# Message passing on one core: twelve of 556 edge tiles fetched row by row on two queues, an earlier merge of the third chunk, and later stores

## The chip, the core and the metric

The kernel runs on one core of a Trainium2 chip. The core has a matrix engine (TensorE, PE in the profile, with PEld for its weight loads), VectorE (DVE), ScalarE (ACT), GpSimd (POOL) and SyncE (SP). Each engine runs its own list of instructions in order and waits for the others by semaphores. SP, ACT and POOL can start DMA transfers; "SPq", "ACTq" and "POOLq" mark what their queues do. The metric is device time in microseconds (us), the median of several runs; lower is better.

## The reference

A graph layer with 12,500 nodes of 128 features and 400,000 edges, sorted by destination. For each edge no longer than 10 a filter is made from its length, multiplied into the projected features of the edge's source node, and summed at its destination; a small network, a residual and a layer norm follow.

```python
rbf = jnp.exp(-(distances[:, None] - centers) ** 2 / (2.0 * width * width))
cut = 0.5 * (jnp.cos(jnp.pi * distances / CUTOFF) + 1.0) * (distances <= CUTOFF)
W = (jax.nn.silu(rbf @ fw1 + fb1) @ fw2 + fb2) * cut[:, None]
messages = (h[src] @ pw + pb) * W
agg = jax.ops.segment_sum(messages, dst, num_segments=num_atoms)
out = h + (jax.nn.silu(agg @ mw1 + mb1) @ mw2 + mb2)
x = _layernorm(x + out)
```

Edge lengths are drawn up to 56, so that most edges fall away.

## The kernel before

**Packing.** The edges are taken in seven chunks (`pack_first`, `pack`). For each chunk VectorE shifts the short edges of each of 128 rows together, POOL scatters them to lists in DRAM (`packed`, line 494), SP reads the lists back (`pair`, `listed`, line 821), and VectorE merges three lists into one (`one_of`, lines 839 and 840). The merged list holds source and place of each edge; TensorE turns it (line 902), and VectorE copies it to `srci` (line 907), the table of source indices. The lengths are merged in `lengths` and stored to `near_d` (line 896). All this is `unpack`.

**Quads.** The 556 tiles of 128 edges that remain are worked in 139 quads of four tiles (`NL = 139`). For a quad: POOL fetches the projected source rows of a tile with one indirect DMA each (`fetch`, line 1048; the first 12 quads fetch `x` itself and are projected later); ACT makes the radial basis (`basis`, lines 1094 and 1095) and a silu (`silu`, line 1109) for a pair of quads, `oct` by `oct`; TensorE multiplies (`first`, line 1103; `second`, lines 1117 and 1120); VectorE multiplies filter and source rows (`message`, lines 1129 and 1131) and builds a one-hot matrix (`place`, line 1143); TensorE sums by destination (`sum_up`, line 1163) and VectorE adds that to the table `aggT` (`add`, line 1196). I call the engines that work on a quad after its fetch "the consumers".

**Tiles by rows.** For the quads in `SINGLY` the first of the four tiles is not fetched by POOL. SP starts 128 DMAs of one 512-byte row each instead (`one_by_one`, line 1038), after reading 32 addresses at a time into registers (line 1034), into one of four slots of `dl_0`.

**Nodes.** From quad 70 on, blocks of four tiles of finished nodes are worked in between (`nodes`): load `x` (line 173), `node_first`, `node_second` (line 1205 and 334), `node_stats`, then for four blocks together `deviations` (a Sqrt on ACT, line 1241) and `scales`, and `normalize` (line 1263 on ACT), which also stores the block on SP (line 173). `tail` and the last lines do this for the last blocks, with `keep_busy` issuing matmuls that nobody reads (line 1352).

**What sets the order.** The order on each engine is written out by the Python code. A planner keeps an estimated time (`clock`), an estimated time of POOL (`pool`, 1.29 us a fetch), and for each chunk the time before which its next step is not put in (`awake`); `pack_until` puts steps of chunks between quads. A row of `one_by_one` is planned at `A_ROW` us. A fetch waits for the sum of a quad four before the newest one written (`FOLLOW`), and for its buffer (`place_of`: 21 buffers at first, for later quads reused after four to six quads).

Of the kernel before, what the change touches and what calls it, by code (L numbers as in the profile page):

```python
# [67 lines left out]
CLEAR_C = 2  # L68
PACK_US = 1.5
EARLY_US = 7  # L70
SINGLY = (22, 45, 62, 67, 86, 102, 118, 133)
A_ROW = .58
AT_ONCE = 32
FROM_BANK = 3


# [7 lines left out]
def kernel(  # L84
# [56 lines left out]

    x_sb, loaded = {}, [0]

    def load_x(t0, n=None):
        t = x4_sb[loaded[0] % X_BUFS]
        loaded[0] += 1
        node_dma(t0, t, x, False, n)
        x_sb[t0] = t
# [293 lines left out]
    def fetches(until, most):  # L442

        while fetched[0] < QT * min(most, known[0]) and pool[0] <= until:
            q, j = divmod(fetched[0], QT)
            fetch(q, table=x if q < FROM_X else None, js=(j,))
            if j == 0:
                pool[0] = max(pool[0], summed.get(before_it(q), 0.0))
            if j or q not in SINGLY:
                pool[0] += 1.29  # L450
            there_at[q] = pool[0] + 2.2
            fetched[0] += 1

    def parts(n):

        return [(a, b) for a, b in ((0, n // 16 * 16), (n // 16 * 16, n)) if b > a]
# [236 lines left out]
    def pack(c):  # L693
# [109 lines left out]
            yield one(n)  # L803

        yield from columns(c, nodes, r_d, first, 0, CAP, at_i)
        awake[c] = pool[0] + (2.2 if c == 1 else 3.0)
        awake[0] = 0.0
        yield 0
        yield from unpack(c)
# [1 line left out]
    def unpack(c):  # L811
# [15 lines left out]
        if c < 2:  # L827
            more_ = np_ if c == 0 else SPILL
            also = work.tile([P, 2, QE], F32, name="s", bufs=3).bitcast(I32)
            listed(also, 0, more_, 3, LISTS)  # L830
        awake[c] = max(awake[c], clock[0]) + (6 if c < 1 else 3.5 if c < 2 else 4.0)
        yield 0
        def alike_in(k):
            nc.vector.tensor_tensor(pair[:more_, :LISTS - 3, k::2], pair[:more_, :LISTS - 3, k::2],
# [2 lines left out]
        def one_of(to, k):  # L837

            nc.vector.tensor_tensor(to, pair[:np_, 0, k::2], pair[:np_, 1, k::2], OP.bitwise_or)
            nc.vector.tensor_tensor(to, to, pair[:np_, 2, k::2], OP.bitwise_or)  # L840
# [49 lines left out]
        def lengths():  # L890

            if c < 2:
                alike_in(1)
            one_of(length, 1)
            for a, b in parts(np_):
                nc.sync.dma_start(near_d[p0 + a:p0 + b], length[a:b].bitcast(F32))
            stored.add(c)

        def to_places(f, to):
            t, tp = turned()  # L900
            for j in range(2):
                nc.tensor.transpose(tp[:, j, :np_], f[:, j * P:(j + 1) * P], ident[:np_, :np_])
            if to is srci:
                lengths()
                yield 1.4 if c < 2 else 0.8
            yield later(-2.0 if c == 1 and to is srci else 0.0)
            nc.vector.tensor_copy(to[:, p0:p0 + np_, :].rearrange("p r j -> p j r"),
                                  tp[:, :, :np_])
            back(t)
# [5 lines left out]
            pool[0] = max(pool[0], clock[0] + 0.4)  # L915
        known[0] = QB[c + 1]
        yield 0
        mine = [q for q in SINGLY if QB[c] <= q < QB[c + 1]]
        if mine:
            at_row = work.tile([64, P], I32, name="at_row", bufs=2)  # L920
            nc.vector.tensor_scalar(at_row[:np_], f_src[:, :P], float(4 * H), None, op0=OP.mult)
            for q in mine:
                p = 2 * (q - QB[c])
                singles.extend((q, e, at_row[p:p + 1]) for e in range(P))
# [100 lines left out]
    def one_by_one():  # L1025

        row_at[0] = max(row_at[0], clock[0] - 8.0)
        while singles and row_at[0] < clock[0]:
# [4 lines left out]
            if e % AT_ONCE == 0:  # L1033
# [5 lines left out]
                              proj.rearrange("n f -> (n f)").bitcast(U8)[ds(rows_at[e % AT_ONCE], 4 * H)]  # L1039
                              .rearrange("(o f) -> o f", o=1))  # L1040

    def fetch(q, idx=None, table=None, js=range(QT)):
        got = quad_sb[place_of(q) if q >= 0 else 0]
        for j in js:
            if q in SINGLY and j == 0:
                continue
            i = srci[:, 2 * q + j // 2, j % 2:j % 2 + 1] if idx is None else idx[:, j:j + 1]
            ins = nc.gpsimd.indirect_dma_start(  # L1048
                out=got[:, j, :], out_offset=None, in_=proj if table is None else table,
                in_offset=bass.IndirectOffsetOnAxis(ap=i, axis=0))  # L1050
# [73 lines left out]
    def message(q, js=(0, QT)):  # L1124
        msg = own(q, "msg", 0)
        a, b = js
        if q in SINGLY and a == 0:
            assert q in alone and all(s[0] != q for s in singles)
            nc.vector.tensor_mul(msg[:, 0, :], pu_of[q][:, :H], alone.pop(q))
            a = 1  # L1130
        nc.vector.tensor_mul(msg[:, a:b, :], pu_of[q].rearrange("p (j f) -> p j f", j=QT)[:, a:b, :],  # L1131
                             got_of[q][:, a:b, :])
        if b == QT:
            free.append(pu_of.pop(q))
            got_of.pop(q)
        return msg
# [115 lines left out]
            ready.append((t, r[:, at:], by[:, at:]))  # L1252
            at += len(rows(t))

    def normalize(t0, rs, by, on=(), eng=nc.sync):

        y = x_sb.pop(t0)
        for k, m in enumerate(rows(t0)):
            if k in on:
                nc.vector.tensor_scalar(y[:m, k, :], y[:m, k, :], rs[:m, k:k + 1], by[:m, k:k + 1],  # L1260
                                        op0=OP.mult, op1=OP.add)
            else:
                nc.scalar.activation(y[:m, k, :], y[:m, k, :], AF.Identity, bias=by[:m, k:k + 1],  # L1263
                                     scale=rs[:m, k:k + 1])
        node_dma(t0, y, out, True, eng=eng)

    ready = []

# [25 lines left out]
    assert begin[early[-1]][2] <= NL - 3  # L1294

    def nodes(q):

        if deep:
            scales(*deep.pop())
        for _ in ready[:1 if q < NL - 6 else 2]:  # L1300
            normalize(*ready.pop(0))
        for k, t0 in enumerate(early):
            if begin[t0][0] - 5 == q:
                load_x(t0)
            if begin[t0][2] == q:
                if k % 4 == 0:
                    st_of[0] = statistics()
                node_stats(t0, st_of[0][:, k % 4 * 4:])
                if k % 4 == 3:
                    deep.append(deviations(early[k // 4 * 4:k + 1], st_of[0]))  # L1310
            if begin[t0][1] == q:
                node_second(t0)
            if begin[t0][0] == q:
                node_first(t0)
        for k, t0 in enumerate(TAIL):
            if q == NL - 9 + k:
                load_x(t0)
        if q == NL - 7:
            st_of[3] = statistics()
            node_stats(80, st_of[3])  # L1320
        if q == NL - 4:
            node_stats(84, st_of[3][:, 4:])
        if q == NL - 3:
            node_stats(88, st_of[3][:, 8:])
            dev_of.append(deviations([84, 88], st_of[3][:, 4:]))
            nc.scalar.activation(warm, half_pi, AF.Silu)
        if q == NL - 2:
            node_second(90)
            for k in (1, 2):
                st_of[k] = statistics()  # L1330
            scales(*dev_of.pop(0))
            for _ in (84, 88):
                normalize(*ready.pop(0))
# [3 lines left out]
    def tail(q):  # L1337

        for t0, k in READY.items():
            if q == NL - k:  # L1340
                if t0 == 84:
                    keep_busy(8)
                assert done_to(2 * added(q + 1)) >= (t0 + TAIL[t0]) * P
                node_first(t0)
            if q == NL - k + 1 and t0 in (80, 84, 88):
                node_second(t0)
# [142 lines left out]
    for q in range(NL - 1):  # L1489
# [3 lines left out]
        if q == NL - 2:  # L1493
            bases_of(q, NL)
        nodes(q)
        most[0] = room(q)
        fetches(clock[0], most[0])
        fetches(math.inf, min(NL, q + AHEAD + 1))
# [30 lines left out]
        for k in now:  # L1529
            if q < NL - 2:  # L1530
                base_of(k, (1,))
            if q == NL - 7 and k == now[0]:
                deep.append(deviations([80], st_of[3]))
                nc.scalar.activation(warm, half_pi, AF.Silu)
            add(k)
# [143 lines left out]
```

## Time and profile before

| | |
|---|---|
| median of 3 runs | 734.89 us (734.77 to 734.94) |
| the profiled execution | 736.03 us |
| its span, first to last instruction | 734.3 us |
| mean granted TensorE clock | 0.92 |
| DMA, mean | 124 GB/s, 91.37 MB |
| rows started on SP for the tiles by rows | 1024 |
| indirect fetches on POOL (lines 1048), and scatters (line 494) | 548 and 7 |

In the rows of a profile, "L1048 POOL DMA_INDIRECT quad<-proj,srci" is an operation of POOL written at line 1048, with what it writes on the left and what it reads on the right; names stand without buffer numbers, so `quad`, `msg` and `hot` are tiles of which there are several. A timeline row gives the start, the time from start to end of a group of alike instructions (x4: four of them), and in brackets the idle time before it and what ended that. Rows of windows give a stretch, its length, and for each engine the busy time and in brackets the number of instructions. Two records of TensorE stand for one f32 matmul of 128 columns.

### The profile page before, as it was taken

To read this page: it belongs to the slowest core of one execution; us is meant where nothing else is said; L and a number is where in the kernel's file an instruction comes from. 1 tells how busy PE (TensorE), PEld (TensorE's weight loads), DVE (VectorE), ACT (ScalarE), POOL (GpSimd) and SP (SyncE) were. 2 spreads that over 40 slices of the span, in tenths; PEclk is the share of its full clock that TensorE was granted. 3 is DMA by queue.
4 is the path that set the end of the run, shared out by engine and by line. 5 is a ranking of instruction groups with operands and counts; after the bars stand their busy time and mean duration, and the time that the engine had idled before them with its cause. 6 is when DMAs were issued, how large, how long until landed. Compare 5 with 4: busy or idle time off the path is not lost.

```text
span 734.3 us, 13663 instructions
## 1 busy us (share of the span) xinstructions
PE 590.7 (80%) x3527; PEld 461.9 (63%) x3527; DVE 560.2 (76%) x1737; ACT 403.0 (55%) x574; POOL 533.5 (73%) x569
## 2 busy tenths in 40 slices
PE   6877876797888787878698969999978787778684
PEld 5766565676666665667476758777656565565463
DVE  8899798878878997989889957877455555556663
ACT  6557634274444864536457256859456644653763
POOL 7777777577777777777777777777777777777750
PEclk9999687999999998989989989999998999999886
DMA  8995442233234323343233343535333433343231
GB/s 267 313 318 189 143 128 73 89 120 99 76 110 128 95 85 101 99 127 88 83 111 113 96 134 97 155 120 151 110 113 94 127 124 98 98 142 116 79 114 53
DMA packets 53103, 91.37 MB, mean 124 GB/s; under 512 B 13824, under 2 KB 20576, under 8 KB 53018
## 3 DMA queue, kind: packets, MB, share of 16 engines
q1 hardware_dynamic: 34466, 53.20, 21.8%
q0 software_dynamic: 17840, 36.77, 18.1%
q8 instruction: 29, 0.48, 0.3%
q10 hardware_dynamic: 712, 0.46, 0.2%
q14 instruction: 56, 0.46, 0.2%
HBM read 74.59 MB, written 15.79 MB: 123 GB/s over the span
## 4 chain that ended last, share of the span: by engine, by line
DMA 13%; PE 13%; DVE 11%; POOL 9%; issue 6%; ACT 3%; DVEq 1%; POOLq 0%; SPq 0%; ACTq 0%
DMA quad<-proj,srci 11%; POOL quad L1048 9%; PE ph L1103 3%; PE bank L1120 3%; PE sums L1163 3%; DVE hot L1143 2%; DVE quad L1143 2%; PE bank L1205 1%; DVE msg L1131 1%; DMA pair<-packed 1%; DVE aggT L1196 1%; DVE st L1230 1%; DVEq L1173 1%; ACT x L1263 1%; DMA packed<-line,at_i 1%
## 5 line engine op out<-in xcount | busy, mean ns | idle before, releaser
L1048 POOL DMA_INDIRECT quad<-proj,srci x421 | 400.9, 952 | 132.5 <-issue 94.9
L1120 PEld LDWEIGHTS bank<-fw_sb,s 128*128 128x128 f32 x1112 | 159.7, 207 | 72.9 <-issue 65.8
L1109 ACT ACTIVATE s<-ph 128x1024 f32<-128x1024 f32 x70 | 71.2, 1017 | 179.7 <-PE ph L1103 179.5
L1120 PE MATMUL bank<-fw_sb,s 128*128 128x128 f32 x1112 | 159.7, 291 | 0.0
L1103 PE MATMUL ph<-rbf,w_sb 102*128 102x512 f32 x278 | 145.9, 651 | 6.7 <-ACT s L1109 3.5
L1163 PEld LDWEIGHTS sums<-hot,msg 128*128 128x128 f32 x816 | 107.6, 198 | 55.9 <-issue 27.5
L1143 DVE TENSOR_SCALAR hot<-iota_n,dl,cut 128x80 f32<-128x80 f32 (+4 forms) x408 | 109.1, 341 | 27.5 <-PE sums L1163 25.3
L1163 PE MATMUL sums<-hot,msg 128*128 128x80 f32 (+4 forms) x816 | 110.4, 280 | 14.2 <-DVE msg L1131 13.9
L1117 PE MATMUL bank<-fb_b,ones_b 96*128 96x512 bf16 x139 | 56.5, 406 | 54.8 <-DVE msg L1131 34.1
L1048 POOL DMA_INDIRECT x<-proj,srci x79 | 75.5, 955 | 24.2 <-issue 19.8
L1131 DVE TENSOR_TENSOR msg<-bank,quad 128x512 f32<-128x512 f32 (+1 forms) x82 | 55.5, 677 | 45.9 <-DMA quad<-proj,srci 41.6
L1103 PEld LDWEIGHTS ph<-rbf,w_sb 102*128 102x128 f32 x278 | 52.6, 211 | 46.1 <-issue 38.3
L1196 DVE TENSOR_TENSOR aggT<-aggT,sums 128x80 f32 (+4 forms) x209 | 53.9, 258 | 32.4 <-PE sums L1163 11.1
L1094 ACT ACTIVATE rbf<-d,rbf_bias,rbf_scale 102x512 f32<-102x512 f32 x70 | 56.3, 804 | 19.6 <-DMA d<-near_d 19.6
L1048 POOL DMA_INDIRECT quad<-in_x_dram,srci x48 | 46.7, 974 | 15.7 <-issue 11.9
L334 PEld LDWEIGHTS bank<-pw_sb,xT 128*128 128x128 f32 (+1 forms) x292 | 43.0, 212 | 9.4 <-issue 6.0
L1109 ACT ACT_TABLE_LOAD x36 | 46.2, 1283 | 0.6
L1095 ACT ACT_TABLE_LOAD x35 | 44.9, 1283 | 0.6
L1095 ACT ACTIVATE rbf<-rbf 102x512 f32<-102x512 f32 x70 | 44.1, 630 | 1.5
L334 PE MATMUL bank<-pw_sb,xT 128*128 128x128 f32 (+1 forms) x292 | 43.3, 296 | 0.7 <-ACT xT L984 0.6
L1163 PE MATMUL sums<-quad,quad 128*128 128x128 f32 (+3 forms) x296 | 40.8, 284 | 2.9 <-DVE quad L1131 2.8
L1143 DVE TENSOR_SCALAR quad<-iota_n,dl,cut 128x128 f32<-128x128 f32 (+3 forms) x148 | 40.6, 353 | 3.3 <-issue 2.1
(272 smaller groups left out, 791.4 us busy)
## 6 DMA issues: line engine op xcount, KB each, us to landing
d<-near_d SPq DMA_DIRECT2D x70, 256.0 KB
dl<-proj SPq DMA_DIRECT2D x1024, 0.5 KB
x<-in_x_dram SPq DMA_DIRECT2D x46, 256.0 KB
quad<-proj,srci POOLq DMA_INDIRECT x421
proj<-hp SPq DMA_DIRECT2D x24, 256.0 KB
out_dram<-x SPq DMA_DIRECT2D x22, 256.0 KB
r_d<-in_edge_weight_dram SPq DMA_DIRECT2D x5, 256.0 KB
r_dst<-in_dst_dram SPq DMA_DIRECT2D x5, 256.0 KB
```

Of the source, the lines that this page charges most:

```text
L334: nc.tensor.matmul(to[:m, k, :], lT[:, k * P:k * P + m], w, start=False, stop=(k == a + c - 1))
L1048: ins = nc.gpsimd.indirect_dma_start(out=got[:, j, :], out_offset=None, in_=proj if table is None else table, in_offset=bass.IndirectOffse ...
L1094: nc.scalar.activation(rbf[:u], d[:u], AF.Square, bias=rbf_bias[:u], scale=rbf_scale[:u])
L1095: nc.scalar.activation(rbf[:u], rbf[:u], AF.Exp, scale=-1.0 / (2.0 * width * width))
L1103: nc.tensor.matmul(ph[:, h, :], w1_sb[:2 * KR, h, :], rbf[:2 * KR], start=True, stop=True)
L1109: nc.scalar.activation(s[:, :n], ph[:, :n], AF.Silu)
L1117: nc.tensor.matmul(pu, ones_b[:, :P], bias_b["fb2"].rearrange("k j f -> k (j f)"), start=True, stop=False)
L1120: nc.tensor.matmul(pu[:, j * H:(j + 1) * H], s[:, j * P:(j + 1) * P], fw2_sb, start=False, stop=(j == QT - 1))
L1131: nc.vector.tensor_mul(msg[:, a:b, :], pu_of[q].rearrange("p (j f) -> p j f", j=QT)[:, a:b, :], got_of[q][:, a:b, :])
L1143: nc.vector.tensor_scalar(hot[:, j, :wide(q)], iota_n[:, :wide(q)], dl[:, at[0], at[1]], cut[:, at[0], at[1]], op0=OP.is_equal, op1=OP.mult)
L1163: ins = nc.tensor.matmul(pa[:, k * W:k * W + wide(q)], msg[:, j, :], hot[:, j, :wide(q)], start=(j % n == 0), stop=(j % n == n - 1))
L1196: nc.vector.tensor_add(to, to, pa[:, k * W:k * W + wide(q)])
```

## The change

- `SINGLY` has nine tiles instead of eight, at other quads; a row is planned at 0.515 us instead of 0.58.
- A second tile (`j = 1`) of quads 45, 87 and 128 (`BESIDE`) is taken from POOL too. `beside`, called at every other quad, starts seven rows on ACT's queue, with the addresses read from `at_beside`. The product of such a quad is made in up to three pieces.
- The third chunk (`c = 2`) takes its next step right after its lists are asked for, and the step after the transposes without delay. For the chunks from the fourth on, the lists are asked for 8 instead of 3 planned us after the scatter, and the store of the lengths is written after the delay, not before it.
- Before quad `NL - 6`, `normalize` does not store; `store_all` does, at the start of the next quad's `nodes` (or before a load into that buffer).
- The last four-block `deviations` and the one of block 80 move from the start of quad `NL - 6` and from quad `NL - 7` to one place behind the sums of quad `NL - 6`; `deep` is emptied in order.
- `keep_busy(8)` at block 84 is gone. Block 90 is normalized on POOL, and 90 and 93 ahead of the last `deviations`.

```diff
-SINGLY = (22, 45, 62, 67, 86, 102, 118, 133)
-A_ROW = .58
+SINGLY = (22, 43, 58, 68, 83, 96, 109, 122, 136)
+A_ROW = .515
+BESIDE = (45, 87, 128)
+BESIDE_ROWS = 7
...
+    def store_all():
+        while to_store:
+            node_dma(*to_store.pop(0), out, True)
     def load_x(t0, n=None):
         t = x4_sb[loaded[0] % X_BUFS]
+        if any(v is t for _, v in to_store):
+            store_all()
...
-            if j or q not in SINGLY:
+            if j != (0 if q in SINGLY else 1 if q in BESIDE else -1):
                 pool[0] += 1.29
...
-        awake[c] = pool[0] + (2.2 if c == 1 else 3.0)
+        awake[c] = pool[0] + (2.2 if c == 1 else 3.0 if c < 3 else 8.0)
...
-        awake[c] = max(awake[c], clock[0]) + (6 if c < 1 else 3.5 if c < 2 else 4.0)
+        awake[c] = max(awake[c], clock[0]) + (6 if c < 1 else 3.5 if c < 2 else 0.0 if c < 3 else 4.0)
...
-            yield later(-2.0 if c == 1 and to is srci else 0.0)
+            yield later((0.0, -2.0, -2.5, *4 * (0.0,))[c] if to is srci else 0.0)
+            if to is srci and c >= 3:
+                store_lengths()
...
+    def beside(n):
+        now, besides[:n] = besides[:n], []
+        while now:
+            q, e, i = now[0]
+            m = sum(1 for v in now if v[0] == q)
+            _, at = nc.values_load_multi_w_load_instructions(
+                i[:, e:e + m], engines=[mybir.EngineType.Activation], min_val=0,
...
+            if e == 0:
+                alone[q] = beside_sb[:, BESIDE.index(q) % 2, :]
+            for k in range(m):
+                nc.scalar.dma_start(alone[q][e + k:e + k + 1, :].bitcast(U8),
+                                    proj.rearrange("n f -> (n f)").bitcast(U8)[ds(at[k], 4 * H)]
+                                    .rearrange("(o f) -> o f", o=1))
+            now = now[m:]
...
-            if q in SINGLY and j == 0:
+            if j == (0 if q in SINGLY else 1 if q in BESIDE else -1):
                 continue
...
+        apart = 0 if q in SINGLY else 1 if q in BESIDE else -1
+        if a <= apart < b:
+            nc.vector.tensor_mul(msg[:, apart, :], pu_of[q][:, apart * H:(apart + 1) * H], alone.pop(q))
+        for a, b in (((a, apart), (apart + 1, b)) if a <= apart < b else ((a, b),)):
...
-        if deep:
-            scales(*deep.pop())
+        while deep:
+            scales(*deep.pop(0))
+        store_all()
         for _ in ready[:1 if q < NL - 6 else 2]:
-            normalize(*ready.pop(0))
+            normalize(*ready.pop(0), soon=q >= NL - 6)
...
-                if k % 4 == 3:
+                if k % 4 == 3 and q != NL - 6:
                     deep.append(deviations(early[k // 4 * 4:k + 1], st_of[0]))
...
-                if t0 == 84:
-                    keep_busy(8)
...
+        if q % 2 == 0:
+            beside(BESIDE_ROWS)
...
-            if q == NL - 7 and k == now[0]:
+            if q == NL - 6 and k == now[0]:
+                deep.append(deviations(early[-4:], st_of[0]))
                 deep.append(deviations([80], st_of[3]))
                 nc.scalar.activation(warm, half_pi, AF.Silu)
...
+    normalize(*ready.pop(0), on=(0, 1, 2), v=nc.gpsimd)
+    normalize(*ready.pop(0))
     last_dev = deviations([95], st_of[2])
-    for _ in (90, 93):
-        normalize(*ready.pop(0))
     scales(*last_dev)
     normalize(*ready.pop(0), on=(0, 1), eng=nc.scalar)
```

More of the change, by code (lines that the diff above doesn't have):

```diff
@@ L142 @@
     x_sb, loaded = {}, [0]
+    to_store = []
+    def store_all():
+        while to_store:
+            node_dma(*to_store.pop(0), out, True)
     def load_x(t0, n=None):
         t = x4_sb[loaded[0] % X_BUFS]
+        if any(v is t for _, v in to_store):
+            store_all()
         loaded[0] += 1
@@ L894, in lengths, with store_lengths @@
             one_of(length, 1)
+            if c < 3:
+                store_lengths()
+        def store_lengths():
             for a, b in parts(np_):
@@ L905, in to_places @@
                 yield 1.4 if c < 2 else 0.8
-            yield later(-2.0 if c == 1 and to is srci else 0.0)
+            yield later((0.0, -2.0, -2.5, *4 * (0.0,))[c] if to is srci else 0.0)
+            if to is srci and c >= 3:
+                store_lengths()
             nc.vector.tensor_copy(to[:, p0:p0 + np_, :].rearrange("p r j -> p j r"),
@@ L917, in unpack @@
         yield 0
[L918 to L924, printed above, removed]
+        for name, some_q, to, j in (("at_row", SINGLY, singles, 0), ("at_beside", BESIDE, besides, 1)):
+            mine = [q for q in some_q if QB[c] <= q < QB[c + 1]]
+            if mine:
+                at_row = work.tile([64, P], I32, name=name, bufs=2)
+                nc.vector.tensor_scalar(at_row[:np_], f_src[:, j * P:(j + 1) * P], float(4 * H), None,
+                                        op0=OP.mult)
+                for q in mine:
+                    p = 2 * (q - QB[c])
+                    to.extend((q, e, at_row[p:p + 1]) for e in range(P))
         part = paired(I32, "part")
@@ L1040, in one_by_one @@
                               .rearrange("(o f) -> o f", o=1))
+    besides = []
+    beside_sb = keep.tile([P, 2, H], F32, name="beside")
+    def beside(n):
[5 more added lines that the diff above has]
+                i[:, e:e + m], engines=[mybir.EngineType.Activation], min_val=0,
+                max_val=(N - 1) * 4 * H, skip_runtime_bounds_check_because=
+                "sources are at most N - 1 where they are copied")
+            if e == 0:
[5 more added lines that the diff above has]
+            now = now[m:]
     def fetch(q, idx=None, table=None, js=range(QT)):
@@ L1126, in message @@
         a, b = js
[L1127 to L1132, printed above, removed]
+        apart = 0 if q in SINGLY else 1 if q in BESIDE else -1
+        if a <= apart < b:
+            assert q in alone and all(s[0] != q for s in singles + besides), (q, len(singles), len(besides))
+            nc.vector.tensor_mul(msg[:, apart, :], pu_of[q][:, apart * H:(apart + 1) * H], alone.pop(q))
+        for a, b in (((a, apart), (apart + 1, b)) if a <= apart < b else ((a, b),)):
+            if a < b:
+                nc.vector.tensor_mul(msg[:, a:b, :],
+                                     pu_of[q].rearrange("p (j f) -> p j f", j=QT)[:, a:b, :],
+                                     got_of[q][:, a:b, :])
+        b = js[1]
         if b == QT:
@@ L1253, in scales, with normalize @@
             at += len(rows(t))
-    def normalize(t0, rs, by, on=(), eng=nc.sync):
+    def normalize(t0, rs, by, on=(), eng=nc.sync, v=nc.vector, soon=True):
         y = x_sb.pop(t0)
@@ L1259, in normalize @@
             if k in on:
-                nc.vector.tensor_scalar(y[:m, k, :], y[:m, k, :], rs[:m, k:k + 1], by[:m, k:k + 1],
+                v.tensor_scalar(y[:m, k, :], y[:m, k, :], rs[:m, k:k + 1], by[:m, k:k + 1],
                                         op0=OP.mult, op1=OP.add)
@@ L1264, in normalize @@
                                      scale=rs[:m, k:k + 1])
-        node_dma(t0, y, out, True, eng=eng)
+        if soon:
+            node_dma(t0, y, out, True, eng=eng)
+        else:
+            to_store.append((t0, y))
     ready = []
@@ L1293 @@
     early = list(begin)
-    assert begin[early[-1]][2] <= NL - 3
+    assert begin[early[-1]][2] == NL - 6
     def nodes(q):
-        if deep:
-            scales(*deep.pop())
+        while deep:
+            scales(*deep.pop(0))
+        store_all()
         for _ in ready[:1 if q < NL - 6 else 2]:
-            normalize(*ready.pop(0))
+            normalize(*ready.pop(0), soon=q >= NL - 6)
         for k, t0 in enumerate(early):
```

## The prediction

> **What bounds the kernel now.** I read the page first (busy shares, costliest groups), then busy times by windows, then POOL's timeline, then the last 60 us of each engine, and last the waits of SP.
>
> ```profile
> span 734.3 us, 13663 instructions
> PE 590.7 (80%) x3527; PEld 461.9 (63%) x3527; DVE 560.2 (76%) x1737; ACT 403.0 (55%) x574; POOL 533.5 (73%) x569
> L1048 POOL DMA_INDIRECT quad<-proj,srci x421 | 400.9, 952 | 132.5 <-issue 94.9
> ...
> 136.00:440.00 304.00, 248.59 (x1492) 194.49 (x1493) 259.82 (x746) 160.28 (x197) 230.52 (x242) 0.93 0.34 104
> 440.00:520.00 80.00, 77.87 (x495) 61.89 (x494) 61.56 (x233) 57.17 (x85) 60.47 (x65) 0.98 0.44 131
> 520.00:690.00 170.00, 137.11 (x791) 101.96 (x790) 96.08 (x318) 89.68 (x121) 128.50 (x136) 0.95 0.36 109
> ...
> 130.54 1.00 POOL L1048 DMA_INDIRECT quad<-proj,srci  x1 [0.30 <-issue]
> 135.96 0.94 POOL L1048 DMA_INDIRECT quad<-proj,srci  x1 [4.42 <-DVE at_row L921]
> 137.21 0.94 POOL L1048 DMA_INDIRECT quad<-proj,srci  x1 [0.31 <-PE bank L982]
> ```
>
> By share PE is busiest (80%), but POOL's 73% is full: between 520 and 690 us it starts 136 fetches in 170 us, one each 1.25 us, the step from 135.96 to 137.21. 0.94 us is busy, 0.30 us falls to "issue" every time. From 136 us on the rate is the same everywhere (242 in 304 us). So every fetch that isn't made is worth 1.25 us, as long as POOL waits for nothing else. It does once: at 130.54 it has fetched the second chunk's last tile, and the next starts 5.42 us later instead of 1.25: 4.2 us lost.
>
> POOL runs ahead first; the consumers catch up. Their rows:
>
> ```profile
> 675.03 0.94 POOL L1048 DMA_INDIRECT quad<-proj,srci  x1 [0.30 <-issue]
> ...
> 677.57 0.69 DVE L1131 TENSOR_TENSOR quad<-bank,quad 128x512 f32<-128x512 f32 x1 [1.20 <-DMA quad<-proj,srci]
> ...
> 708.85 0.95 POOL L1048 DMA_INDIRECT quad<-proj,srci  x1 [0.30 <-issue]
> ...
> 715.16 0.88 DVE L1131 TENSOR_TENSOR quad<-bank,quad 128x128 f32<-128x128 f32 x4
> 720.80 0.61 DVE L1196 TENSOR_TENSOR aggT<-aggT,sums 128x128 f32 x2 [1.04 <-PE bank L1205]
> ```
>
> At quad 131 the product starts 2.5 us after the start of the quad's last fetch (675.03 to 677.57), and VectorE had waited for it: POOL is the bound. At the end it isn't: the last fetch starts at 708.85, so its product could be at 711.4, its sums and the last add near 712.1 (0.2 us for a quarter of 0.88, 0.3 for two matmuls, 0.2 of handing over). That add is at 720.80, so 8.7 us are lost between.
>
> ```profile
> 692.10 1.28 ACT L1241 ACT_TABLE_LOAD   x1
> ...
> 693.72 1.28 ACT L1109 ACT_TABLE_LOAD   x1
> 695.02 0.60 ACT L1109 ACTIVATE s<-ph 128x512 f32<-128x512 f32 x1
> ...
> 695.66 3.57 PE L1352 MATMUL ph<-mb_b,ones_b 96*128 96x512 bf16 x8 [5.54 <-ACT s L1109]
> ...
> 717.20 1.92 PE L1163 MATMUL sums<-hot,msg 128*128 128x128 f32 x8
> ...
> 726.77 1.63 ACT L1263 ACTIVATE x<-x,by,rs 128x128 f32<-128x128 f32 x4
> ...
> 728.31 0.86 ACT L1263 ACTIVATE x<-x,by,rs 128x128 f32<-128x128 f32 x2
> ```
>
> Here they go: at quad 133 a silu stands behind two table loads for a Sqrt, PE stands 5.54 us and then does 3.57 us of `keep_busy`.
>
> **The change, part by part.**
>
> *Fewer fetches.* Twelve tiles off POOL instead of eight: 4 x 1.25 = **-5.0**.
>
> *Third chunk.* The merge now comes right behind the asking.
>
> ```profile
> 116.57 0.77 SPq L821 DMA_DIRECT2D pair<-packed  x2
> ...
> 358.97 3.23 DMA pair<-packed
> ...
> 120.20 0.68 DVE L515 TENSOR_SCALAR bank<-nodes 128x512 int32<-128x512 int32 x1
> ...
> 129.87 0.41 DVE L839 TENSOR_TENSOR two<-pair 44x256 int32<-44x256 int32 x1
> ...
> 124.79 0.36 PE L729 MATMUL bank<-run,ones 128*128 128x1 f32 x2
> ...
> 135.44 0.25 DVE L907 CAST srci<-bank 128x88 int32<-128x88 f32 x1 [0.43 <-PE bank L902]
> ```
>
> The lists are asked for at 116.57 and, with the 3.23 us that another chunk's took, there by 120.6 (second request). In the order by which the code writes the steps, the merge then stands behind the shift step of 120.20, so it starts near 120.9 and waits for nothing; now it starts at 129.87. TensorE reaches the transposes behind line 729, at 125.2, and `srci` is copied near 125.8, where POOL needs it at 131.8. The stall goes: **-4.2**. The wait for the transposes costs VectorE nothing new: it stands there for line 729 already. Late next is the buffer, below.
>
> *Last quads.* Both deviations come after the silu of quad 133 with one Sqrt and one silu load, so PE's 5.54 goes, and 3.57 with `keep_busy`. Together 9.1 us of PE on the path at 690 to 699; what they can give is the 8.7 between POOL and the last add. VectorE can follow: four quads from 704.5 to 715.2 took 3.6 us each, a quad's fetches 5.0. **-8.7**, bounds 0 and -8.7.
>
> *End.* Five scalings run on ACT from 726.77; the last of block 95 ends at 729.2. Three go to POOL, idle by then, and two go ahead of the last Sqrt; the last scale factor is ready with VectorE's scalings at 727.3, so ACT would end at 727.8: **-1.4**. POOL's own time for one isn't in the trace; its nearest 128x128 operation took 0.29 us, so three take about 1 us beside 2 us of other work.
>
> *Rows on SP.*
>
> ```profile
> 250.03 3.13 SPq L1038 DMA_DIRECT2D dl<-proj  x10
> ...
> L1038 SPq DMA_DIRECT2D dl<-proj x1024: 227/228/400, 80.3 to 663.6; - x171
> ...
> L1034 SPq TENSOR_LOAD <-at_row x32: 2050/2162/2358, 77.6 to 648.2; - x32
> ...
> SPq L173 <- ACT x L1263: 58.5, 17, 10.5
> ...
> SPq L821 <- DMA packed<-line,at_i: 26.6, 5, 8.6
> ```
>
> A row takes 0.32 us, with its share of a load of 32 addresses (2.16) 0.39. 128 more rows are 50 us of SP. Against that, stores a quad later spare most of 58.5 us in which SP stood for ACT's scaling, and lists asked for later spare part of 26.6. SP is about even: 0. Behind a late SP stand the lengths `d` of the next basis.
>
> *Rows on ACT.* 384 rows in 57 calls (19 a tile), between quads 6 and 118. No row of ACT's is in the trace.
>
> ```profile
> L1550 ACTq TENSOR_LOAD <-bad_i x1: 703/703/703, 705.6 to 705.6; - x1
> ...
> 729.20 0.58 ACTq L173 DMA_DIRECT2D out_dram<-x  x1
> ...
> 136.00:440.00 304.00, 77.15 (x576) 0.93 0.34 104
> 440.00:520.00 80.00, 22.32 (x168) 0.98 0.44 131
> ```
>
> One address takes ACT 0.70; by SP's slope seven take 1.0. At SP's 0.32 a row, a call is 3.2 us; at ACT's dearest start (0.58, plus 0.09 between) 5.7. A call serves two quads, so 1.6 to 2.9 us a quad. The last two rows are TensorE's sums by window (8 a quad): 72 quads to 440 us, 4.2 us each with 2.2 of ACT; 21 to 520 us, 3.8 each with 2.7 of ACT. With 1.6 ACT has 3.8 of 4.2 and 4.3 of 3.8, later 4.3 of POOL's 5.0. I take 0.32, nearest in kind (one row, one address), and let the calls hide in ACT's idle time but for 440 to 520.
>
> *Buffers.* What POOL gains it must find free:
>
> ```profile
> 436.07 0.42 DVE L839 TENSOR_TENSOR two<-pair 54x256 int32<-54x256 int32 x1 [7.17 <-DMA dl<-proj]
> ...
> 486.93 0.69 DVE L1131 TENSOR_TENSOR quad<-bank,quad 128x512 f32<-128x512 f32 x1
> ...
> 488.38 0.95 POOL L1048 DMA_INDIRECT quad<-proj,srci  x1 [0.32 <-issue]
> ```
>
> Quad 94's first fetch (488.38) goes into the buffer that quad 90's product (486.93, done 487.6) has read: 0.8 us of slack, the least of all. POOL would be there 4.2 + 2 x 1.25 = 6.7 earlier. The consumers must come 5.9 earlier, or POOL stands for the rest. They may: VectorE's 7.17 us (in truth for the seventh chunk's lists, asked for at 432) should go when these are asked for later. ACT's 0.5 us a quad from quad 82 to 90 takes 4 of it back, so 5.9 - 3.2 = 2.7 stay. I take **+3.0**, bounds 0 and 5.9. The extra pieces of products (under 0.4 us at 4 quads) lie in quads that are not the last: 0.
>
> Sum: -5.0 - 4.2 - 8.7 - 1.4 + 3.0 = -16.3. From 736.0 (the profiled execution) 719.7; the median shown is 1.1 lower: **718.6**; I say 719.
>
> By the Trainium skill ("Perfetto Trace Analysis", DMA Instruction, HWDGE) descriptor generation is locked for one sequencer at a time; no run here shows two queues issuing rows together. As a mechanism of this kernel it would be this: a row of ACT's that meets one of SP's waits its 0.23 us out and takes 0.55 instead of 0.32, a call 4.8, ACT 5.1 of 3.8 us a quad from 440 us on, and the buffers' term is at its dear end: 722, to which I give 0.06 of the chance of the first rival below.
>
> By the Trainium skill ("TensorE: Matmul & The Clock Gate", Part 1) the array is throttled unless kept busy for some microseconds. The trace agrees that it is slow at times in the tail (eight sums in 1.92 at 717.20). By that rule the tail without the fillers stays slow: with half rate for some 2 us of matmuls behind the last product, about 721.
>
> **The rivals.**
>
> *Consumers don't come earlier at quads 85 to 96:* POOL stands 5.9: 736.0 - 19.3 + 5.9 = 722.6, as median about 721.5. For it: PE is busy 77.87 of 80 us there. Against: the 7.17.
>
> *The tail stays:* the stall of PE moves to another ACT operation (the scalings of five blocks still lie there). Then only -5.0 - 4.2 - 1.4 and the buffers' 0 to 3: 725 to 728 in the profile's terms, 725 as median.
>
> *ACT becomes the bound (slower).* If a row costs ACT 0.58 and nothing of it hides, ACT has 2.2 + 2.9 = 5.1 us a quad where the consumers take 4.2: 0.9 x 72 = 65 us late by 440 us. The buffers take some 13 (reuse after four quads, 20 us, less the 7 from a quad's first fetch to the end of its product), the gains 19: up to 768. It decides from a call of about 4.7 us (2.2 + 2.35 = 4.55, so 0.35 x 72 = 25, less 13, less the 12 of gains that POOL alone gives: about zero). Halfway, at 5.2 us, 750. Against: ACT stands 179.5 us for `ph`, and rows can fill that.
>
> ```profile
> ACT s L1109 <- PE ph L1103: 179.5, 56, 8.4
> ```
>
> *The merge waits:* the transposes stay behind in PE's queue and `srci` comes no earlier: +4.2, 723.
>
> **How the numbers follow.** Forecast or near it (713 to 722): 0.52. Buffers full, or the merge late (721 to 724): 0.16. Tail stays (724 to 729): 0.14. ACT the bound: 0.12, nearly all slower. Several partial losses, 728 to 735: 0.06, of which a third within 0.2%. A measurement of this kernel tells 0.2% (1.5 us) from no change. So faster 0.86, same 0.02, slower 0.12. The range is 713 (consumers ahead by the whole 7.17 and a little of SP's relief) to 730; outside lie 0.12 slower, some 0.04 between 730 and 735, and 0.03 below.
>
> **What would show it.** POOL: 544 fetches at 1.25 us, no gap near 131 us, last fetch near 702. VectorE's first product of quad 138 within 3 us of its fetch, last add within 4 us of the last fetch. Quads 85 to 96: POOL's idle time there is the buffers' term. ACT: rows at 0.32 us, busy-plus-rows below 4.2 us a quad to 440 us; a wait of PE for `s` that grows shows the slower rival. SP's waits for line 1263 near nothing. I'd be wrong if rows on ACT cost twice SP's, if SP falls behind with `d`, or if PE still stands in the last five quads.

## The result and the profile after

The changed kernel takes 886.6 us (median; 883.6 to 888.5) where the kernel before takes 734.9: 1.206 times as long, 95% interval 1.202 to 1.210. I had forecast 719. The profiled execution took 883.6 us.

The head of the page and its chain of work, after the change:

```profile
span 881.8 us, 14747 instructions
PE 634.6 (72%) x3519; PEld 491.2 (56%) x3519; DVE 564.0 (64%) x1747; ACT 404.3 (46%) x570; POOL 530.3 (60%) x568
...
PE 22%; DMA 20%; ACT 20%; ACTq 12%; SPq 9%; DVE 8%; issue 7%; DVEq 1%; POOL 0%
PE ph L1144 12%; DMA d<-near_d 8%; ACTq L1078 7%; DMA beside<-proj 6%; SPq L1058 6%; ACT s L1150 5%; ACTq L1071 5%; ACT rbf L1135 3%; ACT L1150 3%; PE sums L1208 3%; ACT rbf L1136 2%; PE bank L1161 2%; PE bank L345 2%; SPq L1054 2%; ACT L1136 1%
```

The engines did the work that they did before (VectorE 564.0 us of it instead of 560.2, ACT 404.3 instead of 403.0; TensorE took 634.6 instead of 590.7 for nearly as many instructions), and the span is 147 us longer: for most of that they stood still. POOL, which set the pace before, has 0% of the chain. In its place stand things that were not on it: rows and loads on ACT's queue, rows on SP's queue, the lengths `d`. Busy times by stretch show that the loss isn't at one spot (the last columns are granted clock, DMA share, GB/s):

```profile
440.00:520.00 80.00, 56.14 (x283) 42.53 (x284) 51.07 (x150) 30.69 (x41) 41.62 (x44) 0.81 0.26 76
520.00:690.00 170.00, 122.94 (x670) 92.17 (x668) 93.28 (x336) 74.68 (x104) 95.69 (x101) 0.85 0.32 92
```

POOL starts 101 fetches in 170 us, one each 1.68 us, where it started 136. The granted clock fell with it, 0.85 for 0.95: TensorE stands more, and what it does takes longer (the `ph` matmuls 776 ns on average, 651 before). The groups of waits, by engine first and SP's own queue last (total, times, longest):

```profile
PE ph L1144 <- ACT s L1150: 122.3, 27, 9.8
ACT L1150 <- DMA beside<-proj: 78.2, 20, 7.2
ACT rbf L1135 <- DMA d<-near_d: 71.0, 20, 5.9
POOL quad L1089 <- PE sums L1208: 45.9, 15, 9.0
```

```profile
SPq L1058 <- DMA beside<-proj: 149.8, 71, 8.6
SPq L184 <- ACT x L1308: 13.3, 8, 5.2
SPq L1058 <- DMA d<-near_d: 12.2, 18, 2.5
SPq L1108 <- DMA beside<-proj: 11.2, 7, 3.3
```

TensorE's wait for ACT's silu went from 3.5 us in all to 122.3. ACT in turn stood 71.0 for the lengths `d`, which SP loads (19.6 before). And SP, before it could start a row of its own, stood 149.8 us **for rows of ACT's**. No such wait is anywhere in the code: SP's rows and ACT's rows go to different tiles. The entry "ACT L1150 <- DMA beside<-proj" is no wait for data: it is the time in which ACT's instruction stream was busy issuing the seven rows ahead of line 1150 (in all of its rows together, ACT itself stood some 10 us for a semaphore).

What joins the queues is in the instruction lists. These are SP's, before and after, at about the same place, each with the semaphore that it waits for (DMAHW0 to 7 are the eight that count the transfers of SP and ACT):

```
before   L1038 dl<-proj  waits DMAHW6     after   L1058 dl<-proj  waits DMAHW0
         L1038 dl<-proj  waits DMAHW7             L1058 dl<-proj  waits DMAHW1
         L1038 dl<-proj  waits DMAHW0             L1058 dl<-proj  waits DMAHW2
         L1038 dl<-proj  waits DMAHW1             L1058 dl<-proj  waits DMAHW4
         L1038 dl<-proj  waits DMAHW2             L1058 dl<-proj  waits DMAHW6
```

Each transfer takes the next of the eight, in the order in which the program is written, whichever of the two queues it is for, and waits until the last transfer on that semaphore has landed. With one queue that means: no more than eight in flight. With two, the numbers missing on the right (3, 5) are rows of ACT's; SP's row eight places on must wait until ACT has come to that row, started it, and it has landed. ACT works in order too, behind silus that wait for TensorE. One case, from the timelines of SP (first fence) and of ACT:

```profile
212.51 0.38 SPq L1058 DMA_DIRECT2D dl<-proj  x1
...
215.10 4.11 SPq L1058 DMA_DIRECT2D dl<-proj  x13
```

```profile
212.23 2.92 ACTq L1078 DMA_DIRECT2D beside<-proj  x6
215.19 1.28 ACT L1150 ACT_TABLE_LOAD   x1 [4.78 <-DMA beside<-proj]
```

SP starts a row at 212.51 and the next only at 215.10, though 0.32 us later would do: its semaphore (DMAHW6) was last given to a row that ACT starts at 213.08, and 2.0 us later that has landed. Right away SP starts thirteen in 4.1 us.

This one case stands for all of them. The trace gives the semaphore of each transfer and when each transfer landed. All 71 waits of SP's rows for ACT's rows end within 0.02 us of the landing of the ACT row that was last given the same semaphore. In 32 of them, with 132 of the 150 us, ACT had not even started that row when SP was ready for its own. The transfers themselves are no slower than before: from issue to landing the median is 1.46 us for SP's rows (1.52 before) and 3.31 for the lengths (3.25 before). So it is not that the rows crowd one another on their way.

### The profile page after: what moved, and what is told of

The parts are those of the page before. It is cut to its first block, busy times and chain, and to the rows that moved or that the text cites. A ratio compares the mean times of both kernels' runs of the same rounds, so it can differ in the third digit from the quotient of the medians.

```text
span 881.8 us, 14747 instructions
## 1 busy us (share of the span) xinstructions
PE 634.6 (72%) x3519; PEld 491.2 (56%) x3519; DVE 564.0 (64%) x1747; ACT 404.3 (46%) x570; POOL 530.3 (60%) x568
## 4 chain that ended last, share of the span: by engine, by line
PE 22%; DMA 20%; ACT 20%; ACTq 12%; SPq 9%; DVE 8%; issue 7%; DVEq 1%; POOL 0%
PE ph L1144 12%; DMA d<-near_d 8%; ACTq L1078 7%; DMA beside<-proj 6%; SPq L1058 6%; ACT s L1150 5%; ACTq L1071 5%; ACT rbf L1135 3%; ACT L1150 3%; PE sums L1208 3%; ACT rbf L1136 2%; PE bank L1161 2%; PE bank L345 2%; SPq L1054 2%; ACT L1136 1%
## 5 line engine op out<-in xcount | busy, mean ns | idle before, releaser
L1089 POOL DMA_INDIRECT quad<-proj,srci x416 | 395.5, 951 | 255.8 <-issue 133.6
L1144 PE MATMUL ph<-rbf,w_sb 102*128 102x512 f32 x278 | 178.6, 776 | 137.3 <-ACT s L1150 122.3
L1161 PEld LDWEIGHTS bank<-fw_sb,s 128*128 128x128 f32 x1112 | 163.0, 211 | 46.2 <-issue 40.0
L1144 PEld LDWEIGHTS ph<-rbf,w_sb 102*128 102x128 f32 x278 | 59.0, 235 | 191.4 <-ACT s L1150 127.3
L1161 PE MATMUL bank<-fw_sb,s 128*128 128x128 f32 x1112 | 162.3, 294 | 0.0
L1188 DVE TENSOR_SCALAR hot<-iota_n,dl,cut 128x80 f32<-128x80 f32 (+4 forms) x408 | 111.5, 345 | 75.3 <-PE sums L1208 73.0
L1208 PEld LDWEIGHTS sums<-hot,msg 128*128 128x128 f32 x816 | 125.9, 225 | 47.2 <-issue 41.6
L1208 PE MATMUL sums<-hot,msg 128*128 128x80 f32 (+4 forms) x816 | 123.7, 303 | 0.6 <-DVE msg L1174 0.6
L1150 ACT ACTIVATE s<-ph 128x1024 f32<-128x1024 f32 x70 | 71.3, 1018 | 104.8 <-PE ph L1144 104.5
L1174 DVE TENSOR_TENSOR msg<-bank,quad 128x512 f32<-128x512 f32 (+2 forms) x84 | 54.8, 654 | 9.7 <-PE bank L1161 5.7
L1308 ACT ACTIVATE x<-x,by,rs 128x128 f32<-128x128 f32 (+1 forms) x93 | 37.8, 481 | 9.2 <-DMA beside<-proj 4.9
```

Of the source, the lines that this page charges most:

```text
L1089: ins = nc.gpsimd.indirect_dma_start(out=got[:, j, :], out_offset=None, in_=proj if table is None else table, in_offset=bass.IndirectOffse ...
L1144: nc.tensor.matmul(ph[:, h, :], w1_sb[:2 * KR, h, :], rbf[:2 * KR], start=True, stop=True)
L1150: nc.scalar.activation(s[:, :n], ph[:, :n], AF.Silu)
L1161: nc.tensor.matmul(pu[:, j * H:(j + 1) * H], s[:, j * P:(j + 1) * P], fw2_sb, start=False, stop=(j == QT - 1))
L1188: nc.vector.tensor_scalar(hot[:, j, :wide(q)], iota_n[:, :wide(q)], dl[:, at[0], at[1]], cut[:, at[0], at[1]], op0=OP.is_equal, op1=OP.mult)
L1208: ins = nc.tensor.matmul(pa[:, k * W:k * W + wide(q)], msg[:, j, :], hot[:, j, :wide(q)], start=(j % n == 0), stop=(j % n == n - 1))
```

## The experiments

**The theories.** A: the two queues wait for one another over the shared semaphores, and that is the loss. B, the rival: ACT simply has no time for 57 calls. C: another part of the change is at fault. D, formed later: crossing costs only when ACT is late anyway. The kernel before takes 735 to 738 us on the chips of these runs.

### No rows on ACT

```diff
-BESIDE = (45, 87, 128)
+BESIDE = ()
```

> The changed kernel with the three tiles of ScalarE given back to GpSimd; all else stays. Theory A (the rows of SyncE and of ScalarE wait for one another, because each transfer of either queue waits for an earlier one of the other): 722 us, 715 to 728, which is the predicted 718.6 and three fetches of 1.25. Theory B (ScalarE has no time for 57 calls of some 4 us): also 722. Theory C (another part of the change is at fault): over 760.

Measured: 725.2 us (721.4 to 727.8), 0.984 of the kernel before (0.979 to 0.988). C falls: with those 384 rows gone, the rest of the change is a gain, near the size that the forecast gives for it.

### ACT's time without its rows

```diff
+TIMED = (45, 87, 128)        # the same 57 places; the tiles are POOL's
-            for k in range(m):
-                nc.scalar.dma_start(alone[q][e + k:e + k + 1, :] ...
+            for k in range(10 * m // 7):
+                nc.scalar.activation(beside_sb[:, 1, :], beside_sb[:, 0, :], AF.Copy)
```

> As the run without rows on ScalarE, but at each of the 57 places ScalarE makes ten copies of 128x128 (some 4.1 us, as one load and seven rows take in the changed kernel), and no transfer. Theory A: ScalarE's time alone is not it: within 15 us of the run without these rows, so 722 to 737. Theory B: near the changed kernel, 860 to 890. Between them both count.

Measured: 760.6 us, 35 above the run without rows. Neither A (at most 15) nor B (135 or more). One number of mine was off: a copy took 0.31 us and not 0.41, so a place cost 3.0 us where the changed kernel's calls cost 3.5 (some 200 us over 57 calls, from the end of the instruction ahead of each to the end of its last row). The copies, and the wait that grew:

```profile
L1074 ACT ACTIVATE beside<-beside x546: 292/309/313, 132.9 to 675.9; 128x128 f32<-128x128 f32 x182
```

```profile
PE ph L1138 <- ACT s L1144: 51.3, 24, 5.7
```

ACT had 180 us to spare in the kernel before, in which it stood for `ph`. 168 us of copies put into it cost 35, not 0: idle time of an engine is not one pool. A place that takes 3 us at once, just ahead of a silu that TensorE waits for, is on the path however idle ACT is later.

### The same rows in 12 calls of 32

```diff
-BESIDE_ROWS = 7
+BESIDE_ROWS = 32
-        if q % 2 == 0:
+        if q % 8 == 2:
             beside(BESIDE_ROWS)
```

> The changed kernel with the same 384 rows on ScalarE in 12 calls of 32 (every eighth quad) in place of 57 of at most 7. Theory A: the queues cross 12 times instead of 57, so of some 165 us lost about a fifth is left: 740 to 790. Theory B: the same rows cost ScalarE nearly the same time in larger pieces: 860 or more.

Measured: 830.2 us, between the theories again. With fewer crossings SP's wait for ACT's rows fell from 149.8 to 81.4, but each call now holds ACT for some 13 us, and TensorE stands behind it:

```profile
PE ph L1144 <- ACT rbf L1136: 106.8, 10, 13.2
...
ACT rbf L1135 <- DMA beside<-proj: 60.7, 4, 16.1
```

One loss is traded for another; the run doesn't separate A and B by itself.

### ACT's rows without SP's

```diff
-SINGLY = (22, 43, 58, 68, 83, 96, 109, 122, 136)
+SINGLY = ()
```

> The changed kernel with no tiles on SyncE's rows (its nine tiles go back to GpSimd), while ScalarE keeps its three tiles in 57 calls. Nine fetches more are 11 us for GpSimd. Theory A: the row transfers of ScalarE now follow mostly its own, so the loss goes: 735 to 770. Theory B: ScalarE has the same work as in the changed kernel: 870 to 900.

Measured: 812.6 us, between. To be held against no rows on either queue (734.5, below), it is 78 us, half of the 161 that the same ACT rows cost beside SP's nine tiles (725.2 to 886.6). So half of the loss needs SP's rows as well. Without rows of its own SP still crosses, with the loads of the lengths, at line 1108, but ACT no longer waits for them:

```profile
SPq L1108 <- DMA beside<-proj: 81.8, 16, 7.4
```

The queues wait the other way round too: by the semaphores of the trace ACT's rows stood 22 us for transfers of SP's, in 15 waits.

### One unused row on ACT's queue

The deciding run: crossings without ACT's time. POOL keeps the three tiles; at each of the 57 places ACT starts one transfer, from a fixed address, into a tile that nobody reads.

```diff
-            _, at = nc.values_load_multi_w_load_instructions(...)
-            for k in range(m):
-                nc.scalar.dma_start(alone[q][e + k:e + k + 1, :] ... ds(at[k], 4 * H) ...
+            nc.scalar.dma_start(beside_sb[e:e + 1, TIMED.index(q) % 2, :], proj[e:e + 1, :])
```

> One unused row per place, on a chip on which the kernel before takes its 735 us. Crossing by itself costs (A): 780 to 860. Crossing costs only where ScalarE is also late (D): 725 to 740.

Measured: 794.5 us, 1.081 of the kernel before (1.074 to 1.088). A's range holds it, D's doesn't: 57 transfers of 512 bytes, 13 us of ACT (0.23 each), cost 69 us. SP's waits, and what comes of them on ACT:

```profile
SPq L1059 <- DMA beside<-proj: 84.9, 30, 8.0
```

```profile
ACT rbf L1127 <- DMA d<-near_d: 165.5, 39, 9.3
```

SP stands 85 us for ACT (in 17 of the 30 waits, with 74 us, ACT had not started its transfer yet), and the lengths behind its rows come late: ACT waits 165.5 us for them (44.5 without the extra transfer).

### Copies and one unused row

Both edits at the 57 places, ten copies and then the one transfer.

> Ten copies and one unused row at each of the 57 places. Copies alone cost 35 us, one row alone 69. If the two are separate costs: 725 + 35 + 69 = 829, 815 to 840. If they feed one another (a later ScalarE makes each crossing longer): 845 to 890, near the changed kernel. If one hides in the other: 795 to 810.

Measured: 899.0 us, 1.219 of the kernel before (1.212 to 1.226), a little slower than the changed kernel and just above the range for costs that feed one another (845 to 890). Apart the two cost 35 and 69; together 174. They feed one another:

```profile
SPq L1059 <- DMA beside<-proj: 179.0, 42, 10.2
```

```profile
PE ph L1138 <- ACT s L1144: 129.5, 26, 13.2
...
ACT rbf L1129 <- DMA d<-near_d: 105.9, 23, 9.1
```

They are the waits of the changed kernel (149.8, 122.3, 71.0 there), and longer. ACT comes later to its transfer, so SP stands longer; SP comes later to the lengths, so ACT stands longer. It is a circle of two in-order queues, and it needs no 384 rows: 57, with ACT's time beside them, do.

### No rows at all, ten tiles on SP, eight tiles on SP

Three runs without rows on ACT ask what SP's rows are worth. `SINGLY` is empty in the first, has ten evenly spread tiles and `A_ROW = .46` in the second, and the eight tiles and `.58` of the kernel before in the third.

> No rows on either queue. Nine fetches of 1.25 us more than the run without rows on ScalarE (725): 736, 731 to 741.

> No rows on ScalarE, ten tiles by SyncE's rows, a row each 0.46 us by the planner. One fetch less: 724 if SyncE keeps up, 727 to 735 if its rows make its stores and the lengths late.

> The run without rows on ScalarE (725.2), with the eight tiles and 0.58 us a row of the kernel before on SyncE; third chunk, tail and later stores stay changed. If only the number of fetches counts: one more, 726.5, 725 to 728. If SyncE is short of time with nine tiles, and the lengths are late for it (ScalarE waits 44.5 us for them with nine tiles, 19.6 in the kernel before): 719 to 724.

Measured: none 734.5 us, eight 724.1, nine 725.2, ten 755.3. Without rows the time is as expected. Eight lies between its two ranges and decides nothing by itself; ten is 20 us above the dearer of its ranges. Eight tiles give 10.3 us, the 8 x 1.25 of their fetches. The ninth gives nothing that can be told, and ten cost 30 us more than nine; they lie at other quads, and the planner puts their rows in faster, so not all of the 30 need be the tenth tile's. The group of ACT's basis shows why (last column: idle time ahead of it, and for what) with none, eight and nine tiles, and the wait with ten:

```profile
L1135 ACT ACTIVATE rbf<-d,rbf_bias,rbf_scale 102x512 f32<-102x512 f32 x70 | 56.1, 801 | 0.1
```

```profile
L1135 ACT ACTIVATE rbf<-d,rbf_bias,rbf_scale 102x512 f32<-102x512 f32 x70 | 56.4, 805 | 44.6 <-DMA d<-near_d 44.5
```

```profile
ACT rbf L1135 <- DMA d<-near_d: 102.7, 32, 8.5
```

The first of these rows is word for word the same with none and with eight tiles. With eight SP keeps up; with nine it is at its limit (ACT stands 44.5 us, and most of that is still covered); with ten, at that pace, it is past it. So the changed kernel brought ACT's rows to an SP that had nothing left to lose, and every stall of SP made `d` late at once.

### The third chunk as before

In the run without rows on ACT, the chunks' delays and the place of the stores of the lengths are put back to those of the kernel before (so the later chunks ask for their lists as early as before, too).

```diff
-        awake[c] = pool[0] + (2.2 if c == 1 else 3.0 if c < 3 else 8.0)
+        awake[c] = pool[0] + (2.2 if c == 1 else 3.0)
...
-        awake[c] = max(awake[c], clock[0]) + (6 if c < 1 else 3.5 if c < 2 else 0.0 if c < 3 else 4.0)
+        awake[c] = max(awake[c], clock[0]) + (6 if c < 1 else 3.5 if c < 2 else 4.0)
...
-            yield later((0.0, -2.0, -2.5, *4 * (0.0,))[c] if to is srci else 0.0)
-            if to is srci and c >= 3:
-                store_lengths()
+            yield later(-2.0 if c == 1 and to is srci else 0.0)
```

> The run without rows on ScalarE, with the steps of the third chunk timed as in the kernel before (its old delays, and the lengths stored where they were). If the early merge is worth what the prediction took for it, GpSimd's wait of 4.4 us near 131 us comes back: 725 + 4.2 = 729, 727 to 732. If the gain was taken back by the buffers later: 724 to 726.

Measured: 731.3 us, 0.990 of the kernel before (0.987 to 0.994), where the early merge gives 0.984 (0.979 to 0.988): 5 to 6 us, by ratios and by medians (the later chunks' times went back too, so not all of it need be the merge). POOL's wait is back, in the timelines of this run and, behind it, of the run with the early merge:

```profile
130.78 1.01 POOL L1087 DMA_INDIRECT quad<-proj,srci  x1 [0.30 <-issue]
137.50 0.95 POOL L1087 DMA_INDIRECT quad<-proj,srci  x1 [5.71 <-DVE at_row L938]
```

```profile
131.14 0.94 POOL L1089 DMA_INDIRECT quad<-proj,srci  x1 [0.30 <-issue]
132.39 0.97 POOL L1089 DMA_INDIRECT quad<-proj,srci  x1 [0.30 <-PE bank L1002]
```

### Runs that say little

Four of these kernels had also run, eight times in all, on chips on which the kernel before itself took 1018 to 1026 us, so that nothing there can be held against the other runs. One unused row took 1066 to 1070 there, copies and row 1115 to 1116, no rows 984, ten tiles 1064; for the first two the expectations were these:

> As the run without rows on ScalarE (725 us), but at each of the 57 places ScalarE starts one transfer of one row at a fixed address that nobody uses: no load, no copies, some 0.3 us a place, 17 us of ScalarE in all. If the crossing of the two queues is by itself what costs (A): 57 crossings stay, so 780 to 860. If crossing costs only where ScalarE is also late (D): 725 to 740.

> The ten copies at each of the 57 places (760.6 us by themselves) and the one fixed row behind them. A and D both: copies and crossing together give most of the loss of the changed kernel, 820 to 890. If the number of rows is what costs, and not the crossing: 760 to 775.

Only the order is the same: no rows is the fastest, copies and row the slowest. What slowed those chips stayed open.

## Why the prediction was wrong

The sum was right in most terms and lacked the one that decided. Without ACT's rows, and with the eight tiles of before on SP, the kernel with the other parts of the change shows the terms singly (the last fetch, the last add, the span, from the timelines and the page of that run):

```profile
703.92 0.95 POOL L1089 DMA_INDIRECT quad<-proj,srci  x1 [0.30 <-issue]
```

```profile
709.12 0.61 DVE L1241 TENSOR_TENSOR aggT<-aggT,sums 128x128 f32 x2 [0.83 <-PE bank L1250]
```

```profile
span 722.1 us, 13644 instructions
```

- *Third chunk*, -4.2: right. The stall near 131 us went, and the last fetch starts 4.9 us earlier (703.92 for 708.85).
- *Buffers*, +3.0 (0 to 5.9): the lower bound held in this run. Nothing of the 4.9 was given back.
- *Last quads*, -8.7: most of it. From the last fetch to the last add it is 5.2 us instead of 11.95, so -6.7; of the 2.0 that are missing, more below.
- *End*, -1.4: -0.5. From the last add to the end of the span it is 13.0 us instead of 13.5. The three scalings on POOL took 1.31 us.
- *Fewer fetches*, -5.0: the price of 1.25 a fetch was right (none to eight tiles: 10.3 us for eight). But the ninth tile on SP gave no gain (725.2 for 724.1), and the three of ACT's had a price far above 1.25.
- *Rows on SP*, "about even: 0": wrong. I weighed 50 us of new rows against waits that would go, as sums over the run. SP's wait for the scaling did shrink (`SPq L184 <- ACT x`: 58.5 before, 27.6 with nine tiles, 13.3 in the changed kernel), but not by the later stores: with them and eight tiles it is 67.6, and 167.3 with none. It shrinks as SP gets more rows and comes later. And rows stand in line ahead of the lengths, and with nine tiles ACT already waits 44.5 us for them. I named the lengths as what stands behind a late SP, and gave them no price.
- *Rows on ACT*: the price of a row was right, the two steps behind it were not.

The rows' price in the changed kernel, by line:

```profile
L1078 ACTq DMA_DIRECT2D beside<-proj x384: 234/235/539, 132.5 to 791.9; - x192
L1071 ACTq TENSOR_LOAD <-at_beside x57: 663/1734/2255, 131.0 to 790.5; - x57
```

A row is 0.235 us, 0.33 from row to row (I took 0.32); seven addresses cost 1.73 (I took 1.0); a call 3.5 us (I took 3.2). **The first failed step is "let the calls hide in ACT's idle time but for 440 to 520"**: at 3.0 us a place, with no transfer at all, it cost 35 us. I compared ACT's busy time a quad with the quad's time, as though a call could lie anywhere in it; it lies ahead of a basis or a silu, and TensorE waits. **The second failed step is a term that wasn't in the sum**: I moved a step past SP's and ACT's queues and asked only what it costs on each. The only meeting of the two that I priced was a lock of 0.23 us a row. That a transfer on one makes the other wait until it has landed (69 us with one transfer a place, 174 with ACT's time beside it) I neither named nor bounded.

Of the rivals, "ACT becomes the bound" had the direction, and the sign named for it showed (TensorE's wait for `s` grew from 3.5 to 122.3 us), but by the wrong way: it was to decide from a call of 4.7 us and to end at 768 at most; the calls stayed at 3.5 and the time came out at 887. The rival from the Trainium skill ("Perfetto Trace Analysis", DMA Instruction, HWDGE), that rows meeting on both queues lock descriptor generation and take 0.55 us, isn't borne out by the rows: 128 of ACT's 384 rows overlap in time with a transfer that SP issues, and their median is 0.235 us, as is that of the other 256. Another sentence of the Trainium skill does bear on it: by "DMA: Bandwidth & Descriptors", Anatomy of one DMA — SWDGE (gpsimd) path, any wait for a semaphore happens on the sequencer that issues the transfer, before it is sent off. The page tells it of GpSimd's path; the trace shows the same for SP's: SP itself stands (149.8 us), and with it all that is behind it.

The clock rival, from the Trainium skill ("TensorE: Matmul & The Clock Gate", Part 1), by which the tail stays slow without the fillers, came true in part. In the run with eight tiles on SP and no rows on ACT the granted clock was 0.50 from 700.6 to 707.4 us, and the last product ends at 706.8. Two groups of eight sums, the first at that clock and the second nearly all at full clock:

```profile
705.82 1.82 PE L1208 MATMUL sums<-hot,msg 128*128 128x128 f32 x8
707.48 1.06 PE L1208 MATMUL sums<-quad,quad 128*128 128x128 f32 x8
```

The difference is 0.8 us of the 2.0 by which the last quads' term fell short; what the rest is, is not shown. The fillers had not kept the clock up either: in the kernel before it was 0.50 from 692.1 to 702.4 us, where the fillers of block 84 ran, and from 716.0 to 719.4, at the eight sums of 1.92. So nothing shows that they were worth their 3.57 us.

**What stays open.** How much of the 161 us is ACT's time and how much the crossing can't be divided, since they feed one another. Why ACT's rows still cost 78 us without SP's rows, where copies of nearly the same time cost 35 beside them, is not shown in full; ACT's 22 us of waits for SP's transfers are a part of it that the copies don't have. And no run takes the shared semaphores away alone, with the same transfers on the same queues: that they are what couples the queues rests on the instruction lists, on the landings that end SP's waits and on the one-row run.

## What to carry to other kernels

Before you move transfers to a second queue, look at what tells the program that a transfer has landed: where both queues draw on one small set of semaphores in program order, a transfer of one can be a wait for the other, and two in-order queues fall into step with the slower. Ask of an idle engine not how much idle time it has, but what waits right behind the place where the new work goes in. And price what stands in line behind a queue (here the lengths) before you fill it: SP took eight tiles for nothing, and with ten the kernel was 30 us slower than with nine.

## What was not expected of the hardware and the program

- 57 transfers of 512 bytes that nobody reads cost 69 us (794.5 for 725.2): not by their bytes, nor by the 13 us of issuing them, but by their place in the rotation of eight semaphores.
- Reading seven addresses into ACT's registers took 1.73 us (median), nearly as much as 32 into SP's (2.16), and one took 0.70.
- Two costs of 35 and 69 us made 174 together (899.0 for 725.2).
